# Routing tokens to experts inside the first phase: slots filled from both ends in a two-layer attention and mixture-of-experts kernel

## The chip, the cores and the metric

One Trainium2 chip; the kernel runs on one of its cores. The metric is the device time of one execution in microseconds (us), lower is better. The engines are TensorE (PE in the profile, with PEld for its weight loads), VectorE (DVE), ScalarE (ACT), GpSimd (POOL) and SyncE (SP, which here only issues DMAs). Each engine works its own instructions strictly in the order in which the program holds them, so a waiting instruction holds up all that stand behind it on its engine.

## The reference, cut to what matters

The input is 32 sequences of 256 tokens with 256 features, 8192 tokens in all. Four blocks follow each other, each with a residual sum. The second is a self-attention with a mixture of 8 experts behind it, and its routing is what the change touches:

```python
x = x + attn_16_heads(modulated_self_attention(x, cond))          # layer 0, first part
x = x + ffn_block(adapter(x, cond))                               # attention, then the experts:
def moe(x, wr, w1, b1, w2, b2):                 # x: T = 8192 tokens, C = 2048 slots per expert
    logits = x @ wr;  probs = softmax(logits)
    top1 = argmax(probs);      m1 = one_hot(top1, 8)
    top2 = argmax(where(m1 > 0, -inf, logits));  m2 = one_hot(top2, 8)
    loc1 = cumsum(m1, axis=0) - 1
    loc2 = cumsum(m2, axis=0) - 1 + m1.sum(0)   # second choices come after all first choices
    m1 = m1 * (loc1 < C);  m2 = m2 * (loc2 < C) # an expert takes at most C tokens
    t1, t2 = the two probabilities, each over their sum
    buf[top1, s1] = x;  buf[top2, s2] = x       # s1, s2: the token's place in its expert
    y = (relu(buf @ w1 + b1) @ w2 + b2) * 0.8   # per expert, 256 -> 1024 -> 256
    return t1 * y[top1, s1] + t2 * y[top2, s2]
x = x + linear_attention(modulated(x, cond))                      # layer 1
x = x + butterfly_ffn(norms_by_tables(x, ids, cond))
```

## The kernel before, in words

**Two phases.** The first phase (`sequence(b, exact)`, once for each of the 32 sequences) does everything up to the layer norm ahead of the experts: a modulated projection, an attention over the 16 heads of each token on VectorE (`head_softmax_attention`), two attentions over the 256 tokens of the sequence (`attention(1, ...)` and `attention(2, ...)`), an adapter, and at its end the router's logits, which ScalarE copies into `L_all` (L1070). The normed tokens go to the DRAM buffer `h2buf`. `L_all` holds them as 64 token tiles of 128 (`NT = 64`), two for each sequence. The second phase routes, runs the experts in 32 blocks of 512 slots (`expert_block`), and then layer 1. The second phase starts with new memory pools, so its weights are loaded only when the first phase has ended.

**How the order is made.** Each piece of work is a generator (a `Part`) that yields the engine it needs and an assumed length, a ring buffer it must get or gives back, or another part to join. `side_by_side` (L91) runs all parts of a phase against these assumed lengths and always issues the step that could start first, with the part's rank (its place in the list) to break ties. What comes out is one fixed order of instructions for each engine. A `yield None, 30.0` only moves the assumed time of a part, and so its place in the orders; on the chip nothing waits for a clock.

**The end of the first phase.** The softmaxes of the first phase are computed without subtracting a maximum. The reciprocals of their sums are kept in `rhead` and `rtok`, and after the last sequence six VectorE instructions (L1095 to L1097) test that all of them are moderate; a sum over partitions on TensorE (L1100) gives one number, every engine loads it (L1105), and a branch runs the first phase again in an exact form if it is not moderate. With these inputs the branch is not taken.

**Routing** (`routing`, first in the second phase) works on all 64 token tiles at once: the two choices (five VectorE instructions each on 128x512 elements, L1183 to L1187, one more for the second, L1182), the counts of each group of 16 tiles (L1204), the place within the expert by matmuls with a triangular matrix and the counts before (L1214, L1217, and L1224 for the second choice, which starts behind all first choices), and the slot number, split in a high part `hi` and a low part `lo`. Then the table from slot to token is built as a product of one-hot matrices: for each choice and each group of 8 token tiles three VectorE instructions (L1288 to L1290: `o1`, `ol`, `oh`), one on ScalarE (L1269) and eight matmuls into `tps` (L1259); 16 such groups in all. `tok` (L1297) is read out of `tps`; it is the index of the gathers that bring an expert's tokens (`xg`, L1438, GpSimd). `gates` and `slots` follow, which the experts' results need later. The expert's two matmuls are `bh` (L1482) and `by` (L1497). `butterflies` on VectorE (`bft`, L1539 and on) and loads of weights run beside all this.

**The start of the first phase.** Styles and demodulations come from `condition_tables`; `demodulation` takes the power of -0.5 on GpSimd, for the first four sequences and then for the other 28 (L217). `adapter_tables` loads two tables (`dgb`, `ugb`), multiplies them with the conditions on TensorE (L398), copies the result on ScalarE (L400) and stores it in DRAM as `gtab`, from which each sequence later loads its adapter weights (L883, L885). The first projection of each sequence is `mm<-xT,w_kwT` (L259), its copy `kk` (L947) starts VectorE's work (`hprod<-kk`, L566).

Of the kernel before, what the change touches and what calls it, by code (L numbers as in the profile page):

```python
# [14 lines left out]
F = mybir.dt.float32  # L15
# [154 lines left out]
def network(ctx: ExitStack, tc: tile.TileContext, a: dict, out: bass.AP):  # L170
# [6 lines left out]
    NHI = NSL // P  # L177
# [201 lines left out]
    def demodulation(demod, d2, b0, b1, after=None):  # L379
        if after is not None:  # L380
            yield "join", after
        yield POW, 0.3 + 0.33 * (b1 - b0)
        rsqrt(
            demod[:, b0:b1, :].rearrange("p b m -> p (b m)"), d2[:, b0:b1, :].rearrange("p b m -> p (b m)"),
            2 * (b1 - b0), 1e-8,
        )

    def adapter_tables():

        gsb = yield from get("hp", "gsb", [B, 2 * HID + 2 * D])  # L390
# [74 lines left out]

    rowsA = wA.tile([P, N_ROWS_A], F, name="rowsA")
# [48 lines left out]
    rhead = wA.tile([P, NT, H], F, name="rhead")  # L515
    rtok = wA.tile([P, NT, H], F, name="rtok")
# [15 lines left out]
    vaug_turn = {1: Turns(1), 2: Turns(1)}  # L532

# [384 lines left out]
    def sequence(b, exact):  # L918
# [120 lines left out]
        yield from attention(2, hT, o_n, b, exact)  # L1039
        oT = yield from transposed(o_n, "oT", bias=lambda c: col("bv2", c))  # L1040
# [35 lines left out]
    for l in ("k", "o", "c"):  # L1076
        d2 = wA.tile([P, B, 2], F, name="d2_" + l)
        n = B if l == "c" else N0
        tables[False, l] = Part(condition_tables(l, wT.get(l), sty[l], dem[l], d2, n, 300.0 if l == "c" else 0.0))
        if l != "c":  # L1080
            tables[True, l] = Part(demodulation(dem[l], d2, n, B, tables[False, l]))
    constants_part, adapter_part = Part(constants()), Part(adapter_tables())
    with tc.manual_schedule():
        side_by_side(
            [tables[False, "k"], *(Part(sequence(b, False)) for b in range(B)), tables[False, "o"], constants_part]
            + [tables[True, "k"], tables[True, "o"], adapter_part, tables[False, "c"], Part(numbers())],
            LAGS_A,
        )
# [3 lines left out]
    okay = wA.tile([P, NT, H], F, name="okay")  # L1092
    okmin = wA.tile([P, 2], F, name="okmin")
    for i, r in enumerate((rhead, rtok)):
        nc.vector.tensor_scalar(okay, r, 1e-20, None, ALU.is_ge)  # L1095
        nc.vector.scalar_tensor_tensor(okay, r, 1e20, okay, ALU.is_le, ALU.mult)
        nc.vector.tensor_reduce(okmin[:, i : i + 1], okay.rearrange("p t h -> p (t h)"), AX.X, ALU.min)  # L1097
    pool, _, _ = rings["mm"]
    ps = pool.tile([P, 2], F, name="mm", tag="mm")
    nc.tensor.matmul(ps[0:1, :], ones[:, 0:1], okmin, start=True, stop=True)  # L1100
    oksum = wA.tile([1, 1], F, name="oksum")
    nc.vector.tensor_reduce(oksum, ps[0:1, :], AX.X, ALU.add)
    again = wA.tile([1, 1], I32, name="again")
    nc.vector.tensor_scalar(again, oksum, 2.0 * P - 0.5, None, ALU.is_lt)
    with tc.If(nc.values_load(again[0:1, 0:1]) > 0):  # L1105
        side_by_side([Part(sequence(b, True)) for b in range(B)], LAGS_A)
# [48 lines left out]
    def flat(x):  # L1155
        return x.rearrange("p t e -> p (t e)")

# [7 lines left out]

    def routing():

        revb = rev.unsqueeze(1).to_broadcast(W3)
        mx = [column(f"mx{k}") for k in range(2)]
        first = [column(f"first{k}") for k in range(2)]  # L1170
        m_ = []
        lg = L_all
        for k in range(2):
            e3 = yield from get("sh", "e3", W3)
            m = yield from get("sh", "m", W3)
            mb = yield from get("sh", "mb", W3, BF)
            m_.append((m, mb))
            if k == 1:
                lg = yield from get("sh", "lg", W3)
            yield DVE2, 3.5 + 0.7 * k  # L1180
            if k == 1:
                nc.vector.scalar_tensor_tensor(lg, m_[0][0], -3.0e38, L_all, ALU.mult, ALU.add)  # L1182
            nc.vector.tensor_reduce(mx[k], lg, AX.X, ALU.max)  # L1183
            nc.vector.tensor_tensor(e3, lg, bc(mx[k]), ALU.is_equal)
            nc.vector.tensor_tensor(e3, e3, revb, ALU.mult)
            nc.vector.tensor_reduce(first[k], e3, AX.X, ALU.max)
            nc.vector.tensor_tensor(m, bc(first[k]), revb, ALU.is_equal)  # L1187
            yield back("sh")
            if k == 1:
                yield back("sh")  # L1190
            yield ACT, 0.6
            nc.scalar.copy(mb, m)


        v_, hi_, lo_, cnt = [], [], [], []
        for k in range(2):
            m, mb = m_[k]
            cps = yield from get("mm", "cnt", [P, NSB])
            c_ = wD.tile([P, NSB], BF, name=f"cnt{k}")
            cnt.append(c_)  # L1200
            yield PE, 0.4
            for n in range(NSB):
                w = min(SLAB, NT - n * SLAB) * NE
                nc.tensor.matmul(  # L1204
                    cps[:w, n : n + 1], flat(mb)[:, n * P : n * P + w], oneb, start=True, stop=True
                )
            yield DVE, 0.2
            for n in range(NSB):
                w = min(SLAB, NT - n * SLAB) * NE
                nc.vector.tensor_copy(c_[:w, n : n + 1], cps[:w, n : n + 1])  # L1210
            yield back("mm")
            loc = yield from get("mm", "loc", [P, NT * NE])
            yield PE, 1.5
            nc.tensor.matmul(loc, utb, flat(mb), start=True, stop=False)  # L1214
            for n in range(NSB):
                w = min(SLAB, NT - n * SLAB) * NE
                nc.tensor.matmul(  # L1217
                    loc, c_[:w, n : n + 1].to_broadcast([w, P]), before[:w, n, :], start=False,
                    stop=(k == 0 and n == NSB - 1),
                )  # L1220
            if k == 1:
                for n in range(NSB):
                    w = min(SLAB, NT - n * SLAB) * NE
                    nc.tensor.matmul(  # L1224
                        loc, cnt[0][:w, n : n + 1].to_broadcast([w, P]),
                        e8b[:w].unsqueeze(1).to_broadcast([w, NT, NE]), start=False, stop=(n == NSB - 1),
                    )
            e3 = yield from get("sh", "e3", W3)
            s_ = column(f"s{k}")

            ex, w_, si = column(f"ex{k}"), column(f"w{k}"), column(f"si{k}", I32)
            hii, loi = column(f"hii{k}", I32), column(f"loi{k}", I32)
            hi, lo = column(f"hi{k}", BF), column(f"lo{k}", BF)
            yield DVE, 3.0
            nc.vector.tensor_tensor(e3, loc.rearrange("p (t e) -> p t e", e=NE), m, ALU.mult)
            nc.vector.tensor_reduce(s_, e3, AX.X, ALU.add)
            nc.vector.tensor_scalar(ex, first[k], -float(CAP), float(NE * CAP - 1), ALU.mult, ALU.add)

# [28 lines left out]
        def by_place(ol, oh, o1, n, w, before):  # L1267
# [3 lines left out]
            if before is not None:  # L1271
                yield "join", before
# [1005 lines left out]
```

## Time and profile before

| | us |
|---|---|
| median of 3 runs | 3851.96 (3851.49 to 3854.46) |
| the profiled execution, its own time | 3854.15 |
| its span, first to last instruction | 3852.4 |
| PE busy | 3517.1 (91%) |
| DVE busy | 2513.5 (65%) |
| ACT busy | 1798.6 (47%) |
| POOL busy | 1806.1 (47%) |

The span is 1.75 us shorter than the execution's own time, and that execution was 2.19 us slower than the median. The page tells time as busy shares and as a chain of waits; the rows of a table by stretches of time (busy time of each engine in each stretch, number of instructions in brackets, granted TensorE clock as a share of full speed, share of the DMA engines) tell which engine sets the pace in which stage. A row of a timeline gives start, length, engine, line, operation, and in square brackets how long the engine was idle before and what ended that.

### The profile page before, as it was taken

To read this page: it belongs to the slowest core of one execution; us is meant where nothing else is said; L and a number is where in the kernel's file an instruction comes from. 1 tells how busy PE (TensorE), PEld (TensorE's weight loads), DVE (VectorE), ACT (ScalarE), POOL (GpSimd) and SP (SyncE) were. 2 spreads that over 40 slices of the span, in tenths; PEclk is the share of its full clock that TensorE was granted. 3 is DMA by queue.
4 is the path that set the end of the run, shared out by engine and by line. 5 is a ranking of instruction groups with operands and counts; after the bars stand their busy time and mean duration, and the time that the engine had idled before them with its cause. 6 is when DMAs were issued, how large, how long until landed. Compare 5 with 4: busy or idle time off the path is not lost.

```text
span 3852.4 us, 55376 instructions
## 1 busy us (share of the span) xinstructions
PE 3517.1 (91%) x21996; PEld 2576.6 (67%) x21997; DVE 2513.5 (65%) x4271; ACT 1798.6 (47%) x2714; POOL 1806.1 (47%) x1291
## 2 busy tenths in 40 slices
PE   3899999999999999866999999999898999999999
PEld 2566666666666666543666666666786888888888
DVE  7999998999899999428764641000337556565654
ACT  2677777777777777643222222222332333333333
POOL 3346543544544444414546665553116556565553
PEclk7899999999999999988999999999998999999999
DMA  1001000010000000013323343322342333232321
GB/s 63 15 31 33 30 30 27 24 34 21 30 30 30 30 30 24 24 36 128 100 67 95 101 92 73 63 42 45 102 157 63 102 91 114 84 103 91 121 91 42
DMA packets 136495, 241.43 MB, mean 63 GB/s; under 512 B 19266, under 2 KB 80898, under 8 KB 133667
## 3 DMA queue, kind: packets, MB, share of 16 engines
q0 software_dynamic: 48128, 100.77, 10.7%
q1 hardware_dynamic: 87954, 136.51, 10.6%
q8 instruction: 176, 2.88, 0.3%
q14 instruction: 93, 0.75, 0.1%
q10 hardware_dynamic: 144, 0.52, 0.0%
HBM read 187.25 MB, written 50.48 MB: 62 GB/s over the span
## 4 chain that ended last, share of the span: by engine, by line
PE 38%; DVE 6%; issue 5%; POOL 4%; DMA 1%; ACT 0%; SPq 0%; POOLq 0%; DVEq 0%; ACTq 0%
PE by L1497 10%; PE bh L1482 10%; PE do L2121 4%; PE mm L2056 4%; PE dh L2107 3%; PE mm L267 3%; PE mm L247 1%; PE mm L259 1%; DMA rrows<-ysb,row 1%; PE gram L1671 1%; POOL xg L1438 1%; DVE st L316 1%; POOL ga L1944 1%; PE mm L1448 1%; DVE v L2019 1%
## 5 line engine op out<-in xcount | busy, mean ns | idle before, releaser
L811 ACT ACTIVATE pt<-sc 128x2048 f32<-128x2048 f32 x256 | 481.1, 1879 | 169.5 <-PE sc L802 166.5
L217 POOL TENSOR_TENSOR n<-n,negh 128x32 f32<-128x32 f32 x64 | 376.4, 5881 | 207.5 <-DVE n L663 158.3
L217 POOL TENSOR_TENSOR rstd<-rstd,negh 128x2 f32<-128x2 f32 x160 | 145.7, 912 | 677.2 <-DVE rstd L318 672.7
L1497 PE MATMUL by<-w,hid 128*128 128x256 f32 x2048 | 452.7, 379 | 2.6 <-DVE ysb L1503 2.6
L1482 PE MATMUL bh<-ehT,w 128*128 128x512 f32 x1024 | 451.6, 594 | 2.7 <-DVE ysb L1503 1.6
L1471 ACT ACTIVATE hid<-bh,cols 128x512 f32<-128x512 f32 x256 | 174.9, 688 | 591.0 <-PE bh L1482 537.0
L1497 PEld LDWEIGHTS by<-w,hid 128*128 128x128 f32 x2048 | 386.5, 190 | 66.3 <-issue 13.9
L784 PE MATMUL av<-pt,vaug 128*32 128x256 f32 x4096 | 280.6, 392 | 86.3 <-ACT pt L811 76.7
L1482 PEld LDWEIGHTS bh<-ehT,w 128*128 128x128 f32 x1024 | 194.5, 191 | 223.0 <-issue 214.9
L1503 DVE TENSOR_TENSOR ysb<-by,b 128x512 f32<-128x512 f32 x64 | 44.1, 688 | 455.8 <-PE by L1497 337.7
L1405 POOL DMA_INDIRECT rrows<-ysb,row x128 | 216.5, 1691 | 264.8 <-DMA rrows<-ysb,row 151.5
L622 DVE TENSOR_TENSOR hprod<-hprod 128x1024 f32<-128x1024 f32 (+2 forms) x384 | 319.4, 832 | 6.5
L802 PE MATMUL sc<-qT,kT 32*128 32x256 f32 x4096 | 299.4, 407 | 10.2 <-ACT pt L811 9.1
L614 DVE TENSOR_TENSOR hprod<-hex,kk 128x2048 f32<-128x2048 f32 x128 | 296.2, 2314 | 0.0
L802 PEld LDWEIGHTS sc<-qT,kT 32*128 32x128 f32 x4096 | 188.3, 187 | 108.1 <-issue 88.0
L784 PEld LDWEIGHTS av<-pt,vaug 128*32 128x32 f32 x4096 | 108.2, 110 | 214.4 <-ACT pt L811 120.0
L2107 PE MATMUL dh<-zT,w_eff 128*128 128x256 f32 x1024 | 237.8, 381 | 6.7 <-DVE zT L2084 6.7
L1438 POOL DMA_INDIRECT xg<-h2buf,tok x128 | 149.2, 1166 | 189.4 <-DVE tok L1297 61.3
L2121 PE MATMUL do<-w_con,gT 128*128 128x256 f32 x1024 | 232.2, 381 | 0.0
L2107 PEld LDWEIGHTS dh<-zT,w_eff 128*128 128x128 f32 x1024 | 190.5, 191 | 31.4 <-DVE zT L2084 7.9
L2121 PEld LDWEIGHTS do<-w_con,gT 128*128 128x128 f32 x1024 | 193.6, 191 | 25.6
L571 DVE TENSOR_REDUCE hex<-hprod 128x64 f32<-128x1024 f32 (+1 forms) x192 | 176.1, 948 | 2.4
(613 smaller groups left out, 7119.8 us busy)
## 6 DMA issues: line engine op xcount, KB each, us to landing
w<-in_w SPq DMA_DIRECT2D x16, 1024.0 KB
x<-rrows SPq DMA_DIRECT2D x64, 256.0 KB
bfw<-in_upw SPq DMA_DIRECT2D x10, 1024.0 KB
bfw<-in_dnw SPq DMA_DIRECT2D x10, 1024.0 KB
xT<-in_xT SPq DMA_DIRECT2D x32, 256.0 KB
x<-in_x SPq DMA_DIRECT2D x32, 256.0 KB
ugbb<-gtab SPq DMA_DIRECT2D x32, 256.0 KB
h2buf<-xh SPq DMA_DIRECT2D x32, 256.0 KB
```

What stands on the lines that cost most here:

```text
L217: nc.gpsimd.tensor_tensor(o, o, negh[:p].to_broadcast([p, n]), ALU.pow)
L614: nc.vector.tensor_tensor(pr.rearrange("p j (h d) -> p j h d", d=DH), weights(t, j0, 8)[:, 0].unsqueeze(3).to_broadcast([P, 8, H, DH]), wi ...
L622: nc.vector.tensor_tensor(pr[:, :n], pr[:, :n], pr[:, n : 2 * n], ALU.add)
L784: nc.tensor.matmul(av[32 * i : 32 * i + 32, c % 2, :], va[:, kc, 4 * c + i, :], pt[:, i, kc, :], start=(kc == 0), stop=(kc == 1),)
L802: nc.tensor.matmul(sc[:, i, kc, :], kT[r, m, kc * P : (kc + 1) * P], qT[r, e, m, :], start=True, stop=nm is None,)
L811: nc.scalar.activation(pt, sc, AF.Exp, scale=1.0 / math.sqrt(DH))
L1405: nc.gpsimd.indirect_dma_start(rrows[:, :], bass.IndirectOffsetOnAxis(ap=row[:, j0 + t : j0 + t + 1], axis=0), y[:, t, :], None, compute_o ...
L1438: nc.gpsimd.indirect_dma_start(xg[t], None, h2buf[:, :], bass.IndirectOffsetOnAxis(ap=tok[:, j : j + 1], axis=0))
L1482: nc.tensor.matmul(ps, w["w1"][:, c, f * P : (f + 1) * P], hT[c], start=(c == 0), stop=(c == 1))
L1497: nc.tensor.matmul(ps[:, t, :], hid[f // 4][:, f % 4, (t0 + t) * P : (t0 + t + 1) * P], w["w2"][:, f, :], start=(f == 0), stop=(f == 7),)
L2107: nc.tensor.matmul(ps[:, g, :], w_eff[:, c, f * P : (f + 1) * P], zT[:, c, :], start=(c == 0), stop=(c == 1))
L2121: nc.tensor.matmul(ps[:, t, :], gT[:, f, t * P : (t + 1) * P], w_con[:, f, :], start=(f == 0), stop=(f == 7))
```

## The change

Second choices no longer start behind all first choices of their expert: they are placed from the expert's last slot downwards. So a token's slot depends only on the tokens before it and not on the total. A slot holds a first choice if its place is below the expert's number of first choices; otherwise it can hold a second choice. The one-hot products keep two halves (`tps[:, k]`, one for each choice), and `late` picks between them for every slot.

With that the work is split. `routed_early` joins the first 28 sequences and then routes their 56 token tiles inside the first phase, and keeps the product in `early`. After the branch `routing` does the same for the last 8 tiles alone, adds `early`, and picks. `moderate` tests the sums in five pieces, four of them (28 sequences) as soon as their sequences have answered, the last one of 128x256 elements at the end. `adapter_tables` gets `yield None, 30.0` at its start, and the demodulation of the last 28 sequences 40.0. The new parts stand behind the sequences in the list of parts.

```diff
-    def demodulation(demod, d2, b0, b1, after=None):
+    def demodulation(demod, d2, b0, b1, after=None, at=0.0):
         if after is not None:
             yield "join", after
+            yield None, at
...
     def adapter_tables():
 
+        yield None, 30.0
         gsb = yield from get("hp", "gsb", [B, 2 * HID + 2 * D])
...
+    LATE = 2 * min(4, B)
...
+    def choices_of(a, b):
...
+        for k in range(2):
+            e3 = yield from get("sh", "e3", shape)
+            if k == 1:
+                l2 = yield from get("sh", "lg", shape)
+                yield DVE2, 0.1 + W * 0.0095
+                nc.vector.scalar_tensor_tensor(l2, mk[0], -3.0e38, lg, ALU.mult, ALU.add)
+                lg = l2
...
+            for n in range(5):
+                yield DVE2 if n in (1, 2, 4) else DVE, 0.1 + W * 0.0095
...
+    def places_of(a, b):
...
+        step = 2 if 2 * W * NE <= 512 else 1
+        for k0 in range(0, 2, step):
...
+            for i in range(step):
+                nc.tensor.matmul(loc[:, i, :], utb, mbs[:, k0 + i, a * NE : b * NE], start=True, stop=False)
+                for n in range(n1):
+                    nc.tensor.matmul(
+                        loc[:, i, :], cntb[: wide[n], k0 + i, n : n + 1].to_broadcast([wide[n], P]),
+                        before[: wide[n], n, a * NE : b * NE], start=False, stop=(n == n1 - 1),
+                    )
...
+    def tokens_of(a, b, wide, into):
...
+        for k, (op, at) in enumerate(((ALU.add, NE * CAP - 1), (ALU.subtract, (NE + 1) * CAP))):
+            nc.vector.scalar_tensor_tensor(f[:, 1, k], firsts[:, k, a:b], -float(CAP), nth[:, k], ALU.mult, op)
+            nc.vector.scalar_tensor_tensor(i[:, 0, k], f[:, 1, k], float(at), f[:, 0, k], ALU.add, ALU.add)
...
+                oh = yield from get(wide, "oh", [P, w // 2, 2, NHI, 2], BF)
...
+                yield DVE2, 0.08 + 0.067 * w
+                nc.vector.tensor_tensor(o1, numbers_[:, :, :NHI, :], each(hl[:, 0, k, t : t + w], NHI), ALU.is_equal)
+                yield DVE2, 0.08 + 0.067 * w
+                nc.vector.tensor_tensor(ol, numbers_, each(hl[:, 1, k, t : t + w], P), ALU.is_equal)
+                yield DVE2, 0.08 + 0.067 * w
+                nc.vector.tensor_tensor(oh[:, :, 0, :, :], o1, each(ttb[:, a + t : a + t + w], NHI), ALU.mult)
+                last = Part(by_place(ol, oh, o1, k, t, w, last))
+                yield last
...
+    def routed_early(sequences):
+
+        for p in sequences[: B - LATE // 2]:
+            yield "join", p
+        for step in (choices_of, places_of):
+            yield from step(0, NT - LATE)
+        got = []
+        yield from tokens_of(0, NT - LATE, "kk", got)
+        yield DVE, 0.8
+        nc.vector.tensor_copy(early, got[0])
...
         side_by_side(
-            [tables[False, "k"], *(Part(sequence(b, False)) for b in range(B)), tables[False, "o"], constants_part]
-            + [tables[True, "k"], tables[True, "o"], adapter_part, tables[False, "c"], Part(numbers())],
+            [tables[False, "k"], *first_sequences, Part(moderate()), Part(routed_early(first_sequences))]
+            + [tables[False, "o"], constants_part, tables[True, "k"], tables[True, "o"], adapter_part, tables[False, "c"]]
+            + [Part(numbers())],
             LAGS_A,
         )
...
-    for i, r in enumerate((rhead, rtok)):
-        nc.vector.tensor_scalar(okay, r, 1e-20, None, ALU.is_ge)
-        nc.vector.scalar_tensor_tensor(okay, r, 1e20, okay, ALU.is_le, ALU.mult)
-        nc.vector.tensor_reduce(okmin[:, i : i + 1], okay.rearrange("p t h -> p (t h)"), AX.X, ALU.min)
...
     def routing():
...
+        yield from choices_of(NT - LATE, NT)
+        yield from places_of(NT - LATE, NT)
+        counted = Part(ends())
+        yield counted
+        got = []
+        yield from tokens_of(NT - LATE, NT, "big", got)
...
+        nc.vector.tensor_add(both.rearrange("p k a h -> p k (a h)"), got[0], early)
+        yield back("mm")
+        yield DVE2, 1.0
+        nc.vector.tensor_tensor(to, both[:, 1], late.unsqueeze(1).to_broadcast([P, 2, NHI]), ALU.mult)
+        nc.vector.tensor_add(to, to, both[:, 0])
+        yield DVE, 0.3
+        nc.vector.scalar_tensor_tensor(tok, to[:, 0], float(P), to[:, 1], ALU.mult, ALU.add)
```

`ends` (one cast of the counts, four small VectorE instructions and eight small matmuls) makes `late` and `used`. `gates` gets three VectorE instructions more, because the second choice's true place is now its place plus the count of first choices.

## The prediction

> **What bounds the kernel now.** I read the table of stretches first (columns: stretch and length, then busy us and instruction count of PE, PEld, DVE, ACT and POOL, granted PE clock, DMA share, GB/s), because the change touches four separate stages.
>
> ```profile
> 0.00:50.00 50.00, 16.68 (x64) 13.29 (x64) 24.73 (x30) 12.13 (x25) 27.94 (x22) 0.85 0.35 114
> 700.00:750.00 50.00, 48.38 (x421) 32.82 (x418) 46.97 (x75) 38.69 (x55) 23.02 (x12) 1.00 0.09 29
> 1600.00:1680.00 80.00, 63.01 (x623) 40.04 (x620) 17.94 (x51) 43.91 (x53) 17.92 (x18) 0.98 0.06 20
> 1680.00:1727.00 47.00, 28.04 (x196) 17.34 (x194) 8.04 (x19) 15.21 (x21) 3.78 (x4) 0.72 0.07 24
> 1727.16:1746.30 19.14, 6.28 (x21) 2.14 (x22) 13.18 (x39) 1.24 (x2) 0.00 (x0) 0.50 0.89 297
> 1746.30:1775.30 29.00, 17.49 (x120) 11.46 (x120) 29.00 (x51) 18.31 (x16) 0.00 (x0) 0.90 0.21 81
> 1775.30:1793.00 17.70, 6.16 (x34) 3.83 (x35) 13.75 (x33) 2.37 (x5) 10.51 (x10) 0.61 0.22 66
> 1793.00:2707.00 914.00, 908.78 (x3330) 607.65 (x3328) 352.48 (x488) 218.63 (x322) 494.77 (x372) 1.00 0.33 76
> ```
>
> The reader should see: in the middle of the first phase PE and DVE are both full. In its tail (1600 to 1727) nothing is: DVE is busy 26 of 127 us, ACT 59, PE 91. From 1727.16, the first instruction behind the branch, to 1793 DVE leads (all 29.00 of the middle stretch) and PE, which bounds the 914 us of experts behind it, does almost none of their work. So routing's 66 us stand in full on the path, and a us taken from DVE there is a us of the time; in the tail a us of DVE may cost nothing. The groups of the stretch 1726 to 1793 and the chain of waits name the pieces:
>
> ```profile
> L1259 PE MATMUL tps<-oh,ol 128*128 128x256 bf16 x128 | 18.6, 292 | 14.3 <-ACT oh L1269 12.8 <-DVE oh L1290 1.4
> L1269 ACT ACTIVATE oh<-o,prow 128x1024 bf16<-128x1024 bf16 x16 | 18.4, 1148 | 21.2 <-DVE o L1288 21.2
> L1288 DVE TENSOR_TENSOR o<-i8b,hi 128x1024 bf16<-128x1024 bf16 x16 | 10.9, 680 | 0.0
> ```
> ```profile
> 1727.16 0.70 DVE mx L1183
> ...
> 1778.49 0.30 DVE tok L1297
> 1789.59 2.68 DMA xg<-h2buf,tok
> 1793.05 7.23 PE bh L1482 x13
> ```
>
> From the branch to the end of `tok` 51.63 us pass, from there to the first expert matmul 14.3 us (gathers, transposes).
>
> **The change part by part.**
>
> *1. Start.* The timeline shows PE stopped by one small matmul whose table comes late, with the first projection behind it in PE's order:
>
> ```profile
> 9.66 3.60 PE L367 MATMUL mm<-s,w 128*128 128x32 f32 x16
> 18.59 0.61 PE L398 MATMUL mm<-dgb,condT 128*32 128x128 f32 x2 [5.33 <-DMA dgb<-in_dgb]
> 19.12 6.47 PE L259 MATMUL mm<-xT,w_kwT 128*128 128x256 f32 x16
> 25.86 1.89 PE L259 MATMUL mm<-xT,w_kwT 128*128 128x256 f32 x8
> 27.59 2.29 DVE L566 TENSOR_TENSOR hprod<-kk 128x2048 f32<-128x2048 f32 x1 [14.06 <-ACT kk L947]
> ```
>
> The projection's input (the scaled `xT`) was there at 12.83, and `dem_k`, which its copy needs, at 13.85. With the change the `dgb` and `ugb` matmuls stand behind the first three sequences' transposes, their ACT copies behind the same point; the order of DMA issues on SP and POOL is the same as before there, so `gtab` and the tables lose only what PE's delay costs, and the 28 sequences' power on GpSimd is not needed until the fifth. L259 then starts near 13.3: 19.12 − 13.26 = 5.9 us earlier. A rule would make it more. The Trainium skill, "TensorE: Matmul & The Clock Gate", Part 1, says that PE's clock falls to half after an idle window of some 3.4 us and recovers only after as long a busy one. The granted clock alone does not show this in these rows, but the durations fit it: the 16 matmuls after the idle 5.33 us took 6.47/16 = 404 ns each, the next eight 1.89/8 = 236. Without the idle time 16 would take 3.8 instead of 6.47, 2.7 more gained: 8.6 by the rule, 5.9 by rows alone. I take 8, nearer to the rule since the two durations differ for the same operation. DVE begins with L947's copy (14.06 us idle before `hprod`) and runs nearly full from then on, so this is carried to the tail. **−8 (−5 to −9).**
>
> *2. Work put into the first phase.* By their order on the engines, the 56 tiles' choices and all 14 groups stand in the tail, between the last four sequences' scores and outputs, and end where before had about 1670. They bring: on DVE 14 × 3 × 0.60 (448 wide against 0.68 at 512 elsewhere in the group: my estimate for shapes mixed with the same rows) = 25, choices 11 × 0.62 = 7, places and tokens 5; the sums' test, before 6 instructions at the end, now 12 shorter ones (4 × 1.65 + 1.2, about as much in all). On ACT 14 × 1.15 = 16. On PE 14 × 8 matmuls, 1.08 a group where nothing waits = 15, and 4 to 5 for counts and places, 20 in all. DVE has 100 us free in this stretch and ACT 68, so these two cost by being in the way of a link of the chain, not by their sum. The chain is that of the last attentions (scores, exponentials, outputs):
>
> ```profile
> 1628.41 1.15 PE L802 MATMUL sc<-qT,kT 32*128 32x256 f32 x16 [1.47 <-ACT pt L811]
> ```
>
> A group's 1.08 us of matmuls fit in such a gap of 1.47 only when its `oh` is ready; the 1.15 us on ACT stands in line with exponentials. I laid the new orders over the old start times, gap by gap between the score matmuls: of 20 us on PE and 16 on ACT about half falls in gaps. **+9 (0 if all falls in gaps; +20 if all of PE's is paid).** A gain is excluded: nothing leaves this stretch. The okay test at the end was hidden before (`okmin` ended at 1715.46, PE's last output projection at 1715.51) and its sum and the branch, with 5.2 us of idle DVE ahead of `mx`, remain: 0.
>
> *3. Branch to `tok`.* What remains for 8 tiles, with durations from the small rows here (a 128x64 DVE instruction takes 0.23 us, as `si` does) and from PE rows at the low clock that this stretch grants (0.50): choices 11 × 0.25 = 2.75; counts and cast 0.4; places, ten small matmuls, 1.5; `nths` and eight small DVE instructions 2.15; two groups, six one-hots of 0.60 = 3.6; the last eight matmuls 4.66/24 × 8 = 1.55; adding `early` 0.69, `late` twice 0.42, `tok` 0.30. Sum 13.8. The row for the matmuls:
>
> ```profile
> 1748.30 4.66 PE L1259 MATMUL tps<-oh,ol 128*128 128x256 bf16 x24 [4.65 <-ACT oh L1269]
> ```
>
> 51.6 − 13.8 = **−38 (−34 to −40)**; the shorter end if `ends`, which joins ahead of the sum, is late.
>
> *4. `tok` to the first expert matmul.* 14.3 us before. Now a cover is gone: 38 us earlier the gathers meet the weight stream that starts with the second phase (DMA share 0.89 in 1727 to 1746, loads until about 24 us behind the branch; the gathers would issue from 14 to 24 us behind it). GpSimd's rows price that:
>
> ```profile
> 1788.34 0.95 POOL L1438 DMA_INDIRECT xg<-h2buf,tok  x1 [0.30 <-DMA xg<-h2buf,tok]
> 1793.34 1.88 POOL L1438 DMA_INDIRECT xg<-h2buf,tok  x1 [0.30 <-PE mm L1374]
> ```
>
> With quiet DMA engines 0.95, beside transfers 1.4 to 1.9. PE waits for the eighth gather, of which five fall in the stream: 5 × 0.65 = **+3 (0 to +6)**. The first expert's weights are there before: about 24 us behind the branch against 31 for the matmul.
>
> *5. Behind it.* PE is idle 5.2 of 914 us, so the experts only shift. `gates` and `slots` grow by three instructions of 0.7 on a DVE that is 39% busy, needed only when results are combined: 0, with ±5 for the changed orders.
>
> **Sum:** −8 + 9 − 38 + 3 = −34. 3854.15 − 34 = 3820.2 for an execution like the profiled one, which was 2.2 above the median: **3818**. A difference under 0.2%, 7.7 us, counts as none.
>
> **The rivals.**
>
> *B, the tail pays PE and ACT in full* (0.08). If the products always wait for their `oh` as in the groups row (14.3 us idle, 12.8 of it behind ACT), the in-order queues put 20 + 16 = 36 us in the chain in place of 9: 3845. For: sixteen groups already showed that idleness. Against: there DVE had no slack; here it runs ahead of ACT.
>
> *C, the start's gain is lost* (0.07). PE idle there 5.33 us, but the first sequences may be held by later loads. Then 3826. For: between L259 and `kk` stand a copy, transposes and another copy, each of which can wait. Against: none of them waits for a load now.
>
> *D, slower* (0.03). Each of the 14 groups stands wholly in the attention chain: DVE 1.81, ACT 1.15, PE 1.08 in series are 4.04 × 14 = 56.5, with choices and places 11 in series: 67, no gain at the start, 3854 − 2 + 67 − 38 + 3 = 3884, or 3876 with it. It decides when the tail grows by over 43 us, 3.1 us for each group. Against: DVE's part is for `o1` and `ol` independent of attention, and rings of buffers let it run ahead.
>
> *A, the forecast*: 0.82. That the change does not do what it says is excluded for the orders: they show 2 groups behind the branch and 14 ahead.
>
> **The numbers.** The main case's ends are −8 to −9 at the start, 0 to +20 in the tail, −34 to −40, 0 to +6, ±5; ends do not all fall together, so 3802 to 3837 holds the main case and C, and leaves out most of B and D. Faster by over 0.2% are A, C and B's greater part: 0.94; the same, B stretched to the tail's 43 us: 0.03; slower, D: 0.03.
>
> **What would show it.** Right: L259's first matmul near 13.3 with durations near 240 ns; branch about 1 us from the old 1727; `tok` 14 us behind it and `bh` 31; the end of experts shifted by as much as `bh`. Wrong: a branch later than 1740 (B, D; the score rows' idle time would name ACT `oh` work ahead of `pt`), `hprod` still at 27 (C), or POOL's gathers over 2 us each and `bh` over 37 us behind the branch.

## The result, and the profile after

The changed kernel took 3811.8 us (median of 4 runs, 3808.09 to 3816.05) against 3851.72 in the 4 runs of the kernel before that go with it: ratio 0.9897, 95% interval 0.988 to 0.9914, so 33 to 46 us faster. Forecast were 3818 and 34. The profiled execution of the changed kernel took 3813.55 us, with a span of 3811.8; the spans differ by 40.6 us. Cut at the same instructions, both traces give (starts and ends from the timelines):

| part | forecast | before | after | difference |
|---|---|---|---|---|
| start of the span to the first `hprod` | −8 | 27.59 | 22.39 | −5.2 |
| from there to the end of the last router matmul | +9 | 1695.4 | 1697.9 | +2.5 |
| to the first instruction behind the branch | 0 | 4.2 | 3.2 | −1.0 |
| branch to the end of `tok` | −38 | 51.6 | 13.8 | −37.8 |
| end of `tok` to the first `bh` | +3 | 14.1 | 16.4 | +2.3 |
| `bh` to the end | 0 | 2059.6 | 2058.2 | −1.4 |

The start, as the timeline of the changed kernel shows it (start, length, engine, line, operation; in brackets the idle time before):

```profile
10.44 3.60 PE L366 MATMUL mm<-s,w 128*128 128x32 f32 x16
13.85 6.55 PE L258 MATMUL mm<-xT,w_kwT 128*128 128x256 f32 x16
20.67 1.89 PE L258 MATMUL mm<-xT,w_kwT 128*128 128x256 f32 x8
22.39 2.29 DVE L730 TENSOR_TENSOR hprod<-kk 128x2048 f32<-128x2048 f32 x1 [8.10 <-ACT kk L1111]
24.15 0.41 PE L399 MATMUL mm<-dgb,condT 128*32 128x128 f32 x2
```

The wait of 5.33 us for `dgb` is gone and the first projection follows `L366` without a gap. But its 16 matmuls still take 6.55 us, 409 ns each, with no idle time before them.

The stretches (PE, PEld, DVE, ACT, POOL busy us, granted PE clock, DMA share, GB/s) show where the work went:

```profile
1600.00:1680.00 80.00, 74.24 (x707) 50.92 (x705) 47.07 (x107) 56.86 (x69) 18.70 (x16) 0.98 0.06 19
1680.00:1723.48 43.48, 27.04 (x182) 16.55 (x181) 5.41 (x17) 13.04 (x17) 1.97 (x2) 0.64 0.06 20
1723.48:1737.26 13.78, 4.87 (x36) 3.09 (x36) 10.85 (x38) 2.30 (x2) 0.00 (x0) 0.50 0.85 270
1737.26:1753.63 16.37, 4.54 (x13) 2.50 (x14) 11.16 (x30) 2.19 (x3) 11.95 (x12) 0.50 1.01 360
1753.63:2675.00 921.37, 917.54 (x3364) 615.48 (x3364) 354.95 (x493) 220.20 (x324) 494.04 (x372) 1.00 0.33 75
```

In 1600 to 1680 DVE is busy 47 us where it was 18, ACT 57 where it was 44, PE 74 where it was 63, in about the same time: the tables' work lies in what was idle. Routing behind the branch is 13.78 us. The stretch that follows has the DMA engines full (1.01), where the kernel before had 0.22 there: the gathers now run inside the weight stream. The groups of 1723 to 1754 show two one-hot groups left of sixteen, and the wait that leads now, PE's for the gathered rows (GpSimd's 22.3 us are put down to a bias load, but it starts 1.07 us behind `tok`, and 0.97 in the kernel before, so it is `tok` that it waits for):

```profile
L1529 POOL DMA_INDIRECT xg<-h2buf,tok x12 | 12.5, 1041 | 25.7 <-DMA b<-in_b 22.3 <-issue 3.3
L1539 PE MATMUL mm<-ident,xg 128*128 128x128 f32 x12 | 4.6, 457 | 13.8 <-DMA xg<-h2buf,tok 12.7 <-issue 1.1
L576 PE MATMUL tps<-oh,ol 128*128 128x256 bf16 x16 | 3.6, 412 | 4.0 <-ACT oh L585 4.0
```

### The profile page after: what moved, and what is told of

The parts are those of the page before. It is cut to its first block, busy times and chain, and to the rows that moved or that the text cites. A ratio compares the mean times of both kernels' runs of the same rounds, so it can differ in the third digit from the quotient of the medians.

```text
span 3811.8 us, 55412 instructions
## 1 busy us (share of the span) xinstructions
PE 3516.6 (92%) x22001; PEld 2582.0 (68%) x22001; DVE 2519.2 (66%) x4296; ACT 1796.2 (47%) x2714; POOL 1810.6 (48%) x1291
## 3 DMA queue, kind: packets, MB, share of 16 engines
q0 software_dynamic: 48128, 100.77, 10.8%
q1 hardware_dynamic: 87954, 136.51, 10.7%
## 4 chain that ended last, share of the span: by engine, by line
PE 41%; DVE 5%; issue 4%; POOL 3%; DMA 1%; ACT 0%; SPq 0%; POOLq 0%; DVEq 0%; ACTq 0%
PE by L1588 11%; PE bh L1573 11%; PE do L2212 4%; PE mm L2147 4%; PE dh L2198 3%; PE mm L266 3%; PE mm L246 1%; PE mm L258 1%; PE gram L1762 1%; PE mm L1539 1%; DVE st L315 1%; POOL ga L2035 1%; DVE v L2110 1%; DVE hh L2049 0%; POOL gc L2035 0%
## 5 line engine op out<-in xcount | busy, mean ns | idle before, releaser
L1588 PEld LDWEIGHTS by<-w,hid 128*128 128x128 f32 x2048 | 387.6, 191 | 67.2 <-issue 14.4
L1496 POOL DMA_INDIRECT rrows<-ysb,row x128 | 220.5, 1723 | 256.9 <-DMA rrows<-ysb,row 148.5
```

What stands on the lines that cost most here:

```text
L1496: nc.gpsimd.indirect_dma_start(rrows[:, :], bass.IndirectOffsetOnAxis(ap=row[:, j0 + t : j0 + t + 1], axis=0), y[:, t, :], None, compute_o ...
L1588: nc.tensor.matmul(ps[:, t, :], hid[f // 4][:, f % 4, (t0 + t) * P : (t0 + t + 1) * P], w["w2"][:, f, :], start=(f == 0), stop=(f == 7),)
```

## The experiments

All ratios are to the kernel before, run on the same chip beside each kernel. Cut as in the table above (tail: first `hprod` to the end of the last router matmul; experts: first `bh` to the last `by`):

| kernel | first hprod | tail | branch to tok | tok to bh | experts | ratio, 95% interval |
|---|---|---|---|---|---|---|
| before | 27.6 | 1695.4 | 51.6 | 14.1 | 921.3 | 1 |
| changed | 22.4 | 1697.9 | 13.8 | 16.4 | 921.3 | 0.9897 [0.9880, 0.9914] |
| e1 delays alone | 21.0 | 1697.8 | 51.6 | 14.1 | 919.7 | 0.9985 [0.9976, 0.9993] |
| e2 all behind the branch | 21.2 | 1692.7 | 49.9 | 9.6 | 924.5 | 0.9964 [0.9950, 0.9978] |
| e3 no early work | 20.8 | 1704.6 | 13.6 | 22.1 | 924.6 | 0.9925 [0.9908, 0.9941] |
| e4 test at the end | 20.5 | 1701.0 | 13.9 | 17.3 | 921.6 | 0.9910 [0.9893, 0.9926] |
| e5 all other loads later | 20.8 | 1694.7 | 13.8 | 9.6 | 954.1 | 0.9966 [0.9954, 0.9979] |
| e6 warm start, o table later | 26.8 | 1746.1 | 13.8 | 15.6 | 921.9 | 1.0042 [1.0026, 1.0059] |
| e7 four late tiles | 21.5 | 1695.5 | 10.7 | 17.5 | 929.2 | 0.9909 [0.9893, 0.9926] |
| e8 PE filled in the tail | 20.8 | 1707.8 | 13.8 | 16.2 | 921.0 | 0.9926 [0.9909, 0.9942] |
| e9 no early work, same order | 20.6 | 1690.1 | 14.1 | 21.5 | 927.0 | 0.9922 [0.9905, 0.9938] |
| e10 layer 1's weights later | 20.9 | 1694.6 | 13.8 | 14.3 | 938.2 | 0.9943 [0.9927, 0.9960] |
| e11 warm start alone | 17.4 | 1695.3 | 13.8 | 15.7 | 920.3 | 0.9898 [0.9881, 0.9914] |
| e12 warm start, four late tiles | 20.0 | 1697.6 | 10.7 | 17.4 | 929.9 | 0.9906 [0.9890, 0.9921] |

The tails need care: the changed kernel, e5, e10 and e11 have one and the same order from the first `hprod` to the branch, and their tails are 1697.9, 1694.7, 1694.6 and 1695.3. Differences in the tail of some 3 us between single profiles are therefore nothing; the mean of the four is 1695.6. The column covers the whole first phase behind the first `hprod`, not its last stage alone. The first `hprod` varies too: ten kernels have the start of the change (all but the one before, e6, e11 and e12), and theirs came at 20.5 to 22.4. The changed kernel's own profile is the latest of the ten.

**e1, the start alone.**

```diff
 def demodulation(...):
     yield "join", after
+    yield None, 40.0
 def adapter_tables():
+    yield None, 30.0
```

> The kernel before with the two delays alone (adapter_tables 30.0, demodulation of the last 28 sequences 40.0), nothing else of the change. Theory (the changed trace: hprod at 22.39 in place of 27.59, PE's clock full only from 19.63 on): the first hprod at about 22.4, its 16 projection matmuls still 400 ns on the mean because the clock is at half until about 6 us into them, and 5 us less in all, 3847. Rival, the clock gate as the prediction used it: 8 us less, 3844, with those matmuls near 240 ns. Rival C: the gain is lost later, 3852.

The first `hprod` came at 21.02, 6.6 earlier than before, and the time was lower by 0.07 to 0.24% (3 to 9 us). That excludes that nothing is carried. The interval alone does not separate 5 from 8; the projection, which is L259 in this kernel, does:

```profile
13.33 5.70 PE L259 MATMUL mm<-xT,w_kwT 128*128 128x256 f32 x16
```

That is 356 ns each, between the theory's 400 and the rival's 240, and without idle time before it. Single matmuls step at 0.43 us until 17.4 and at 0.22 after, so the clock was at half when they began: the rival is out. How many of the 16 run slowly differs from profile to profile (last section). Of the 6.6 us, 4.1 are left at the branch.

**e2, all routing behind the branch, in the new slots.**

```diff
-    yield from choices_of(NT - LATE, NT)
-    yield from places_of(NT - LATE, NT)
+    yield from choices_of(0, NT)
+    yield from places_of(0, NT)
...
-    yield from tokens_of(NT - LATE, NT, "big", got)
+    yield from tokens_of(0, NT, "big", got)
```

> The changed kernel with all 64 token tiles routed behind the branch, in the new slots: routed_early is gone, routing does choices, places and all 16 one-hot groups. Theory: the gain is that of moving the work, so branch to tok goes back to about 50 us (16 groups at 2.0 us of VectorE and more on ScalarE and TensorE, choices 11 x 0.69), tok to bh back to 14.5, the tail gets back 2 to 3 us; 34 more than with the change, about 3846. Rival: the new slots made routing itself cheaper (places without totals, choices without a cast, one sum), then branch to tok is 40 us or less and the time under 3837.

Branch to `tok` is 49.9 us again: of the 37.8 that the change took from it, 36.1 are work moved and 1.7 cheaper routing. The groups of this stretch are those of the kernel before, ScalarE's included:

```profile
L575 PE MATMUL tps<-oh,ol 128*128 128x256 bf16 x128 | 19.5, 304 | 13.9 <-ACT oh L584 12.7 <-DVE cc L1390 0.7 <-DVE oh L607 0.4
L584 ACT ACTIVATE oh<-o,prow 128x1024 bf16<-128x1024 bf16 x16 | 18.4, 1148 | 29.9 <-DMA w<-in_w 20.1 <-DVE o L603 9.7
```

In all it was slower than the change by some 26 us (0.9964 against 0.9897 of 3852), not 34: its tail was short and `bh` came 9.6 us behind `tok`. The second is one of order: 8 transposes of gathered rows stand before the first `bh` here, 12 in the kernel before and in the changed one, and the last four wait for the second block's gathers.

**e3 and e9, the early work left out.** In e3 the part only fills its tables with zeros (on GpSimd, after the first 28 sequences); in e9 its steps are still taken in the list of parts, with nothing issued, and the tables are filled at the start.

```diff
-    for step in (choices_of, places_of):
-        yield from step(0, NT - LATE)
...
+    yield POOL, 3.0
+    for v in (firsts, nths, tops, mbs, cntb, early):
+        nc.gpsimd.memset(v, 0.0)
```
```diff
-        yield from step(0, NT - LATE)
+        yield from step(0, NT - LATE, Nothing())   # every call of it does nothing
```

> The changed kernel with the routing of the 56 early tiles left out: in place of it a few fills with zeros, so the token table holds only the last 8 tiles. Read at the branch, it prices the work put into the tail. Theory (its matmuls found PE's gaps: in the trace of the change PE is idle 13 us less in the tail for 14 us more work): the branch comes 1.5 to 4 us earlier than with the change, at 1720 to 1722. The prediction's size: 9 us earlier, 1714. Rival B: 27 us or more earlier.

> The changed kernel with the early part's 56 tiles left out again, but with the steps still taken in the list of parts, so that all other instructions of the first phase keep the order that they have in the changed kernel; its tables are filled with zeros at the start. Read at the end of the last router matmul, counted from the first hprod (with the change 1697.9 and, in the kernel with later loads that has the same first phase, 1694.7). Theory (14 groups mostly in gaps): 1689 to 1693, so 3 to 6 us are paid. Rival (the order that the scheduler makes out of the change moves the tail more than the work does): 1695 or more.

e3 went against all theories: with the work gone the tail was longer, 1704.6. The part's other assumed lengths had made another order of the same instructions. With the order kept (e9) it was 1690.1. So the work of the 56 tiles costs 1695.6 − 1690.1 = 5.5 us (4.5 to 7.8 over the four profiles; of e9 there is one profile, which may itself be off by some 3), and the order in which the scheduler puts the rest can cost about 12: of 1704.6 − 1690.1 = 14.4, 2.2 were there 1500 us behind the first `hprod`, before any instruction stands elsewhere. The fills on GpSimd are no rival: in e3 they end at 1544.0, and GpSimd is then idle for 10.5 us. Both theories of e9 hold a part; that the order weighs more than the work was not expected. Stretches of e3 and of e9, in which PE does nearly the same:

```profile
1600.00:1680.00 80.00, 65.12 (x600) 39.98 (x600) 14.87 (x45) 41.24 (x49) 10.01 (x13) 0.89 0.05 15
```
```profile
1600.00:1680.00 80.00, 64.39 (x618) 42.67 (x616) 16.96 (x52) 43.30 (x58) 11.46 (x13) 0.97 0.06 21
```

The mean clock is 0.89 in e3 and 0.97 in e9. That goes with the difference; in 1680 to 1713 it is the other way round, 0.79 and 0.60, and that the clock is the cause is not shown. (Both leave most of the token table at zero, so behind `tok` they gather one row of DRAM over and over, and their last columns say nothing of the change.)

**e4, the test of the sums as before.**

```diff
-    [..., Part(moderate()), Part(routed_early(...))]
+    [..., Part(routed_early(...))]
+for i, r in enumerate((rhead, rtok)):   # behind the list, as in the kernel before
+    nc.vector.tensor_scalar(okay, r, 1e-20, None, ALU.is_ge)
```

> The changed kernel with the test of the sums as before: six VectorE instructions on all 64 tiles behind the list of parts instead of five pieces. Theory: the three on rhead come to stand in the full VectorE near 1530 again and cost their 3.1 us there, the branch 2.5 to 3 us later, about 3815 in all. The prediction's reading (hidden on both sides, the same work in other pieces): within 1 us of the change, 3812.

The timeline of the kernel before had shown the place, and e4 has it again: half of the test does not stand at the end, but in the middle of the last full stretch of VectorE.

```profile
1530.52 0.69 DVE L1095 TENSOR_SCALAR okay<-rhead 128x1024 f32<-128x1024 f32 x1
1531.24 1.23 DVE L1096 SCALAR_TENSOR_TENSOR okay<-rhead,okay 128x1024 f32<-128x1024 f32 x1
1532.50 1.22 DVE L1097 TENSOR_REDUCE okmin<-okay 128x1 f32<-128x1024 f32 x1
1533.64 0.25 DVE L835 RECIPROCAL rtok<-mm 128x16 f32<-128x16 f32 x1
```
```profile
1525.37 0.69 DVE L1260 TENSOR_SCALAR okay<-rall 128x1024 f32<-128x1024 f32 x1
1526.10 1.23 DVE L1261 SCALAR_TENSOR_TENSOR okay<-rall,okay 128x1024 f32<-128x1024 f32 x1
1527.36 1.22 DVE L1262 TENSOR_REDUCE okmin<-okay 128x1 f32<-128x1024 f32 x1
1528.49 0.25 DVE L998 RECIPROCAL rall<-mm 128x16 f32<-128x16 f32 x1
```

In the changed kernel nothing stands between the two reciprocals:

```profile
1527.68 0.35 DVE L771 RECIPROCAL rall<-rall 128x32 f32<-128x32 f32 x1
1528.34 0.26 DVE L999 RECIPROCAL rall<-mm 128x16 f32<-128x16 f32 x1 [0.30 <-PE mm L993]
```

The three hold up the reciprocals behind them by 3.1 us; between before and the changed kernel VectorE's instructions gain 2.9 us at exactly this point. The exponentials of the attentions gain there too, against the kernel before: 2.5 to 2.9 us in the changed kernel and in all of e2, e5 and e7 to e12, and 0.0 in e1 and e4, which have the test in its old place. So the gain at this point is shown. e4's tail is 3.1 longer than the changed kernel's and 5.4 longer than the mean of four, but its other instructions stand in another order too, and in the times (0.9910 against 0.9897) it cannot be told.

**e8, PE filled in the tail.**

```diff
     nc.vector.tensor_copy(early, got[0])
     yield back("mm")
+    ps = yield from get("mm", "mm", [P, P])
+    for _ in range(60):
+        yield PE, 0.24
+        for _ in range(2):
+            nc.tensor.matmul(ps, ident, ident, start=True, stop=True)
```

> The changed kernel with 120 small matmuls more on TensorE (results not used) that fill its assumed gaps from the end of the early routing on. [...] Theory (the clock in the tail costs more than work there): the matmuls take 13 us, yet the clock in 1680 to 1713 rises from 0.64 to over 0.8 and the branch comes 0 to 4 us earlier, 3808 to 3812. Rival (work on PE costs its length in the tail): the branch 8 to 13 us later, 3820 to 3825.

The clock rose as expected, and more, to 1.00, and still the tail was 12.2 us longer than the mean of four (10 than the changed profile), which is the rival's figure.

```profile
1680.00:1713.00 33.00, 29.88 (x289) 25.50 (x288) 2.07 (x8) 12.24 (x15) 1.97 (x2) 1.00 0.05 17
L629 PE MATMUL mm<-ident 128*128 128x128 f32 x240 | 29.2, 277 | 0.0
```

But the fill is 29.2 us of PE and not the 13 of the expectation: each of the 120 float32 matmuls shows as two records, 0.11 us apart. So 10 to 12 of 29 us were paid, not the whole length (by the ratios 11, 0.9926 against 0.9897); a full clock did not pay them back. The fill stands from 1663 to 1708, behind the early groups, of which the last ends at 1659.8. Whether that place makes the difference is put to the test by e7.

**e7, four late tiles in place of eight** (`LATE = 2 * min(2, B)`), **and e12, the same with the matmuls of e11.**

> The changed kernel with LATE at 4 tiles in place of 8: the early part waits for sequence 30 of 32 and routes 60 tiles, 16 groups, in what is left of the tail, about 1645 on. Theory (the work is cheap only where PE and VectorE have gaps and its chain can end before the last sequence's): behind the branch 2 us less, in the tail 3 to 10 us more, 3813 to 3820 in all. Rival (the work is free in the tail wherever it stands): 2 us less, 3810.

> The changed kernel with both the 20 matmuls at the start and LATE at 4: the same order of all else as with LATE at 4 alone. With LATE at 4 the first expert matmul came 4.2 us earlier (from the first hprod), but from it to the experts' end 929.2 us passed in place of 921.3, 10.6 of them PE waiting near 2184 for an ehT that waited for butterfly work on VectorE. Theory (that wait follows from the order that the scheduler made with LATE at 4): 927 to 931 again, 3805 to 3810 in all, no better than the matmuls at the start alone (3804.6). Rival (it was a chance meeting in time): 921, and 3799 to 3802 in all.

The tail did not grow (1695.5; 1697.6 in e12), so the theory of e7 was wrong there. All of its 15 early groups lie where e8 has its fill:

```profile
L576 PE MATMUL tps<-oh,ol x120: 273/275/416, 1673.0 to 1704.7; 128*128 128x256 bf16 x120
```

So it is not a late place as such that costs. Why e8's fill was paid in part and this work was not stays open. Branch to `tok` lost 3.05 us, and the gain was given back in the experts, +7.9. Waits of PE in e7 and in e12 (sum, times, longest), 1740 to 2640 and 1730 to 2690:

```profile
PE bh L1573 <- ACT ehT L1542: 10.6, 1, 10.6
```
```profile
PE bh L1583 <- ACT ehT L1552: 10.8, 1, 10.8
```

In e7 ScalarE's `ehT` waits 18.1 us there for `bfx` of the butterflies, which share a ring of buffers with it. It comes again at the same instruction in e12, which has the same order from the first `hprod` to the branch, so it belongs to the order made with `LATE` at 4 and is no chance meeting.

**e5 and e10, later loads.** e5 starts `last_weights` (layer 1's) and `butterflies` with `yield None, 80.0` and `60.0`; e10 delays `last_weights` alone, by 40.0.

> The changed kernel with the loads of layer 1's weights and of the butterfly matrices started later (their parts begin with assumed delays of 80 and 60), so that on SP they stand behind the store of the gates and only two experts' weights stream while the first gathers run. Theory (with 64 tiles late, where the stream is over before the gathers, tok to bh took 9.6 us; with the change 16.4, its eighth gather landing 5.9 us after its issue): tok to bh about 11, 5 us less in all, 3807. Rival (GpSimd's issue of eight gathers at 1.25 us each and the transposes set it): 1 us or less.

> The changed kernel with the loads of layer 1's weights alone moved behind the store of the gates on SP; the butterfly matrices stay where they were, so the experts' order on the engines is nearly that of the change. Theory (the stream ahead of the gathers is 1.4 MB shorter, about 4 us at 340 GB/s, but w_eff and the first butterfly matrix still run): tok to bh 13 to 15 in place of 16.4, and from bh to the experts' end still 921 to 923; 3809 to 3811 in all. Rival (what lengthened the experts by 33 us with all loads later was these weights): the experts' end 10 us or more later.

In e5 `bh` came 9.6 us behind `tok`, but that mixes two things: the new order also has 8 instead of 12 transposes before it. The stream's own price is in the first transpose, which waits for the first gather; before and with the change:

```profile
1782.83 0.47 PE L1448 MATMUL mm<-ident,xg 128*128 128x128 f32 x1 [6.07 <-DMA xg<-h2buf,tok]
1744.98 0.48 PE L1539 MATMUL mm<-ident,xg 128*128 128x128 f32 x1 [9.69 <-DMA xg<-h2buf,tok]
```

It starts 4.1 us behind `tok` before, 7.7 with the change, 4.3 in e5, 7.5 in e10. GpSimd starts the eighth gather 10.8 to 11.0 us behind `tok` in all four. What both kernels won there they lost in the experts, 33 and 17 us. In e5 PE is idle there 26.2 us in place of 3.8, most of it for the butterflies' results and for `ysb`, which stands behind butterflies on VectorE:

```profile
PE by L1588 <- DVE ysb L1594: 8.3, 1, 8.3
PE mm L1665 <- DVE bfb L1632: 8.1, 1, 8.1
PE mm L1691 <- DVE bfx L1636: 4.5, 1, 4.5
```

For e10 the rival was right, against my theory; of the 16.3 us that PE is idle in the experts, 13.4 are for `ehT`:

```profile
PE bh L1573 <- ACT ehT L1542: 13.4, 2, 10.6
```

What in the order leads to it was not tried.

**e6 and e11, PE busy before its first work.** e11 puts 20 small matmuls first and e6 22 (40 and 44 records in the profile); e6 also starts the table of `o` later, by an assumed 8 us. The diff is e11's.

```diff
+def warmer():
+    sc = yield from get("sc", "sc")
+    for n in (13, 7):
+        yield PE, 0.2 * n
+        for _ in range(n):
+            nc.tensor.matmul(sc[:, 0, 0, :P], ident, ident, start=True, stop=True)
+        yield None, 1.0
+    yield back("sc")
```

> The changed kernel with 22 small matmuls on TensorE ahead of its first real one (their result is not used) and the second style table (o) moved behind the first projection. Theory of the clock [...]: the clock is full by the first projection, its 16 matmuls take 4 us in place of 6.5, and the o table's eight no longer stand ahead of it: first hprod 4 to 6 us earlier than with the change, 3806 in all. Rival (xT's landing and scaling bound it): 1 us or less.

> The changed kernel with 20 small matmuls ahead of TensorE's first real one (results not used) and nothing else: the o table stays where it was. Theory [...]: the 16 matmuls of L366 take about 2 us in place of 3.6, those of the first projection 3.8 in place of 6.5, and from L366's start to the first hprod 8 us pass in place of 11.95; 3808 in all. Rival (the matmuls delay the first styles by as much, or xT is late): no gain, 3812 or more.

e6 was slower than before by 16 us, for reasons outside both theories. The table of `o` still stood ahead of the first projection on PE and its load now came late, the fault that the change had taken away for `dgb`. And the copy of `d_o` fell behind the `hprod` of later sequences on VectorE, and the power of `dem_o` waited for it:

```profile
17.56 1.06 PE L351 MATMUL mm<-condT,aff 128*128 128x32 f32 x4 [6.13 <-DMA aff<-in_oaffT]
POOL dem_o L210 <- DVE d_o L370: 109.9, 1, 109.9
```

e11 has the matmuls alone:

```profile
1.54 7.18 PE L1292 MATMUL sc<-ident 128*128 128x128 f32 x40 [1.54 <-POOL negh L196]
8.55 1.09 PE L351 MATMUL mm<-condT,aff 128*128 128x32 f32 x8
9.90 1.97 PE L366 MATMUL mm<-s,w 128*128 128x32 f32 x16 [0.26 <-DVE s L361]
11.70 3.70 PE L258 MATMUL mm<-xT,w_kwT 128*128 128x256 f32 x16
17.39 2.29 DVE L730 TENSOR_TENSOR hprod<-kk 128x2048 f32<-128x2048 f32 x1 [5.27 <-ACT kk L1111]
```

L366 takes 1.97 in place of 3.60, L258 3.70 in place of 6.55, and the first `hprod` starts 7.5 us behind L366 in place of 11.95. Its profiled span is 3798.2, 13.6 less than the changed kernel's; but its ratio (0.9898) is that of the change (0.9897), since the kernel before was faster in those runs too. So the start is 5.0 us shorter than in the changed profile and 3.1 to 4.1 shorter than in the nine other kernels with that start, and a gain over the change is not shown by the times. No version that beats the change by a clear margin was found.

## Why the prediction was right, point by point

**Right, by its own steps.** Branch to `tok`: 13.8 forecast, 13.78 measured; e2 shows that it is the moving that pays. That it fits to hundredths is luck: from the branch to the end of the places it took 4.07 us for 4.65 forecast, from the last one-hot to the end of `tok` 3.97 for 3.38. `tok` to `bh` +3, measured +2.3; end of the experts unchanged from `bh` on. The total, 40.6 less for 34 forecast, is two errors of opposite sign, 2.8 us too much at the start and 6.5 too little in the tail, and some 3 us of smaller ones. Rivals B and D did not come: the branch was at 1723.5. Two of the signs named for being right did not come either, the first projection near 240 ns and a branch about 1 us from the old one (it was 3.7 earlier).

**The start was over-credited (−8 for −5.2).** The step that failed is the choice of the clock rule over the rows. The Trainium skill ("TensorE: Matmul & The Clock Gate", Part 1) speaks of half the clock after an idle window, and I laid the 404 ns of L259 to the idle 5.33 us. In the changed kernel there is no idle time and they take 409 ns. The clock had not fallen, it had never been up: L367, ahead of the idle time, took 3.60 us, as in the changed kernel, and 1.97 where the clock is up (e11). Single matmuls of L258 step at 0.43 us until 19.6 and at 0.22 after, in the kernel before the same at 24.7. e11 shows the rule itself at work: once PE has been busy with 128-wide matmuls from 1.5 to 6.7 us, their spacing halves, and L258 is quick. The 5.9 of the rows was the better number: in the ten kernels with this start the projection began 5.2 to 6.3 us earlier than before and the first `hprod` 5.2 to 7.1.

The `dgb` wait vanished and what it gave was carried through two thirds of the first phase: the k-th exponential of the attentions stands 4.8 to 5.5 us earlier from 100 to 1217 us in the two traces. Then the lead fell to 2.1 to 2.4 us, in two windows of 3.41 us at half clock, from 1214.3 and from 1231.4, which the kernel before does not have at these exponentials. The first of them and the same work before:

```profile
1214.30:1217.71 3.41, 3.41 (x27) 1.73 (x31) 3.14 (x4) 2.07 (x4) 1.18 (x2) 0.50 0.00 0
1219.50:1223.00 3.50, 3.39 (x40) 2.16 (x40) 3.38 (x5) 2.76 (x5) 1.43 (x2) 1.00 0.02 5
```

So a part of the loss that rival C names came, though not through loads. That these windows are the cause is not shown by an experiment.

**The tail was over-charged (+9 for +2.5).** Two terms were mis-sized. The 56 tiles' work cost 5.5 us (e9), not 9. And the test, put at 0 as "about as much in all", gave 2.5 to 2.9: the lengths were about equal (7.6 us in 15 instructions, not 12, for 6.3 in 6), but the place was left out. Half of it stood at 1530 on a full VectorE, which the timeline of before shows; so "nothing leaves this stretch", which excluded a gain, was wrong. The two do not add up to the row, because the row holds more: in the exponentials, counted from the first `hprod`, the changed kernel lost 2.8 us up to 1500, above all in the two windows at half clock, gained 2.6 at the test and lost 2.3 behind it. With the mean of the four profiles the row would be +0.2. The lesson of that step is that a sum of equal lengths is 0 only between places that are equally busy.

**Right total, wrong reason in `tok` to `bh`.** I had priced GpSimd's issue at 1.4 to 1.9 us a gather inside the stream. It issues as fast as before (1.09 us on the mean of the first eight, 1.08 before); the first gather lands later, 7.7 us behind `tok` in place of 4.1, and part of that is caught up by the eighth. So +3 for +2.3 was luck in its reason.

## What to carry to other kernels

Work moved out of a serial stretch can cost little in a stage whose engines wait for each other, here 5.5 us where it had taken 36, and even late in that stage (e7). The idle share alone does not promise it: of e8's 29 us of matmuls, put where PE looked idle, 10 to 12 were paid. In a kernel whose order is written by assumed times, any edit reshuffles the rest, and an order can cost more than the work (about 12 us against 5.5 here), so a part should be priced with the order held fixed. Before a sum of removed and added instructions is called even, look up in the timeline where each stood.

## What the runs showed of the hardware

**The start is at half clock until PE has had wide work.** In the changed kernel PE is nearly always busy from 9.56 us on with matmuls that are 32 wide, and the clock rises only at 19.6, after some 6 us of 256-wide ones (the clock column of a stretch ahead of its first record, which is at 19.6, reads 1.00; the lengths of the matmuls tell the truth there, 634 ns at half clock and 379 at full). So a busy PE in the profile is not what the clock goes by. In all traces here the granted clock changes only at steps of 3.41 us, which fall differently on the program in each execution. So in the ten kernels with this start the clock rose 2.6 (e3) to 5.8 us (the changed kernel) behind the first 256-wide matmul: a step with 2.58 us of them was followed by the full clock (e3, 13.05 to 16.46), one with 2.37 was not (changed kernel, 12.81 to 16.22), though PE was busy all through both. That is why the length of the start is in part chance. In e12 the clock was up at 6.1, fell again at 12.9 behind a step with 32-wide matmuls in which PE was busy 2.41 us, and came back at 16.3; L258 took 5.39 us there.

**A step of 3.41 us that is half empty can be enough to halve it.** Cut at the changes of the granted clock, the changed kernel's tail reads:

```profile
1661.43:1664.84 3.41, 3.41 (x44) 2.02 (x44) 1.26 (x2) 0.82 (x2) 0.00 (x0) 1.00 0.00 0
1664.84:1668.26 3.42, 1.95 (x28) 1.01 (x28) 0.00 (x0) 2.32 (x3) 0.00 (x0) 1.00 0.02 5
1668.26:1671.67 3.41, 1.78 (x13) 0.98 (x9) 2.92 (x11) 0.31 (x1) 0.35 (x1) 1.00 0.00 0
1671.67:1675.08 3.41, 3.17 (x11) 2.62 (x12) 0.92 (x3) 1.86 (x4) 1.63 (x2) 0.50 0.00 0
1675.08:1678.50 3.42, 3.42 (x17) 3.01 (x17) 1.96 (x6) 0.53 (x2) 1.34 (x2) 1.00 0.00 0
```

After two steps with PE 57 and 52% busy the clock is at half for one, and back after one that was 93% busy. It is not a fixed threshold in the busy time that the profile shows. In all 14 traces together, of the steps at full clock with PE busy under 40%, all 214 were followed by half clock; of those at 50 to 60%, 22 of 267; of those over 80%, none of 13114. Of the steps at half clock, none of 534 under 75% was followed by the full one, and 272 of 274 over 95% were.
